# Router scores as extra columns of A's products, and z of the next group ahead of out of this one

## The chip, the cores and the metric

The kernel runs on one core of one Trainium2 chip. The metric is the device time of one execution in microseconds; lower is better. Its engines are TensorE (PE in the profile; its weight loads are listed apart as PEld), VectorE (DVE), ScalarE (ACT), GpSimd (POOL) and SyncE (SP, which here only starts DMAs). Everything is computed in 32-bit floats.

## The reference

`x` has the shape (64, 64, 1024): 64 samples, each a matrix of 64 rows (c) by 1024 columns (t). Each sample picks one of 16 matrices of 64x64. The result of that product goes through a mixture of 64 low-rank experts, 16 of them per token, and is added to x.

```
W   = weights[condition]                       # (64, 64, 64)
xf  = einsum('bct,bcd->bdt', x, W)             # conditioned rows, 4096 x 1024
scores = xf @ Wr.T                             # 4096 x 64
top_vals, top_idx = top_k(scores, 16)
G   = scatter(softmax(top_vals))               # gates, 0 where not chosen
h   = einsum('nd,krd->nkr', xf, A)             # 64 experts of rank 16 = 1024 columns
out = einsum('nkr,kdr->nd', h * G[:, :, None], B)
return x + 2.0 * out
```

The product with W works on the rows of a sample, A and Wr on the columns. So the kernel may multiply x by A first (the product is called z here) and put W on afterwards; for the scores it may do the same with Wr.

## The kernel before, in words

The 4096 rows are worked in 8 groups of 512 (four tiles of 128 rows, `TPG = 4`). A group has two large products, each 512 x 1024 by 1024 x 1024:

- z = x A (called "h" in the code, L582 on), by blocks `a_t` that stay in SBUF,
- out = h B (called "o"), by blocks `b_t`.

Each product is done by a Strassen-Winograd scheme: seven products of quarters, p1 to p7, instead of eight. They are called parents, and `parent()` makes one. At level 1 a parent is 16 matmuls of 512 columns. At level 2 each parent is itself split into seven leaves, of two matmuls each, 128 x 128 by 128 x 256. A 32-bit matmul appears in the trace as two records (passes). Group 0 is at level 1, z of group 1 has two parents at level 1 and five at level 2, and all else is at level 2. A leaf of B, and some of A's (p4, p6, p7), is computed once, written to DRAM while group 0 runs, and fetched again for every use into a ring of `RING` = 14 buffers. `mm()` (L482) issues a leaf's two matmuls and then `fetch()`, which starts the next fetch on SP's queue and waits there until the buffer is free. Leaves p1, p2, p3, p5 of A stay in SBUF. The parents' order within a product is ORDER: z goes p1 p2 p4 p6 p7 p5 p3, out goes p1 p7 p4 p6 p5 p2 p3.

`run()` (L496) writes out one parent. Its order on PE is: p1 into bank x, p2 into bank y, p3 of the parent before (the "tail"), p6 into x, p4 of the parent before, the hooks "mid", the left sums of the parent after (`prepare`, four DVE sums), the hooks "late", p7 into bank w, p5 into x, then `done` of the parent before and the hooks "end". Bank x is copied by ACT on the way (l_r after p1, l_a after p6, l_b after p5), because each of these partial sums is needed by another quarter (`copied`, L513), and `part` (L517) adds such a copy to another bank on DVE. `done` adds the finished parent to the others on DVE: for z the sums of quarters (`z_parents`), for out the addition to the residual tile, and the store of a quarter when it has all its parts.

The order of everything is written by hand (`manual_schedule`). `at(n, when, f)` hangs a step f on a hook of parent n. The steps that matter here:

- Scores. `scores_t` (L167) multiplies Router's columns (`wr_sb`) by the group's x tiles: 16 matmuls of 256 columns into `st`. `turn` (L186) brings the result to rows (four matmuls, `sp`), `scores` (L198) puts W on it (eight matmuls of 64x64, `sw`). Each has one bank of the pool `ps_s`, and one copy on ACT. The group's scores are made in the out stage of the group before: `scores_t` in its third parent, `turn` in its fourth, `scores` in its fifth.
- Routing. `route_top`, `exps` and four `rest` steps choose the 16 largest and form the exponentials. `scaled` is four ACT activations that scale them, `gates` four PE transposes (`gp`) and a copy into `gg`.
- `gated` (L284) puts W on one quarter of z: 64 records of 64x64 matmuls into two banks (`zp`), then two DVE products with the gates into `hb`, the left operand of out. The four quarters come one by one in four different parents: the fifth and the seventh of z, the first and the second of out.
- `load_x` fetches a quarter of the next group's x (512 KB); all four stand after the first parent of out. `load_res` fetches the four residual tiles, in the third parent of z (the fifth in group 1).

SBUF tiles are in pools; while group 0 runs, a part of SBUF holds the B blocks and the staging tiles, and `second_level()` gives it to the ring and the temporary tiles of the leaves (`lp`, `lt`). PSUM has 8 banks: 7 in the pool `acc`, 1 in `ps_s`. The order of the stages is z0 out0 z1 out1 z2 out2 .. z7 out7.

Of the kernel before, what the change touches and what calls it, by code (L numbers as in the profile page):

```python
# [15 lines left out]
P = 128  # L16
# [8 lines left out]
RING = 14  # L25
# [3 lines left out]
def kernel(  # L29
# [22 lines left out]

    nc = tc.nc
# [3 lines left out]
    KR = a_t.shape[1] * a_t.shape[4]  # L57
# [12 lines left out]
    mp = ctx.enter_context(tc.tile_pool(name="mp", bufs=5))  # L70
    rp = ctx.enter_context(tc.tile_pool(name="rp", bufs=4))
    acc = ctx.enter_context(tc.tile_pool(name="acc", bufs=7, space=PSUM))
    ps_s = ctx.enter_context(tc.tile_pool(name="ps_s", bufs=1, space=PSUM))
# [3 lines left out]
    bpool = first_group.enter_context(tc.tile_pool(name="bpool", bufs=1, side="right"))  # L77
    bsum = first_group.enter_context(tc.tile_pool(name="bsum", bufs=4, side="right"))
# [15 lines left out]
    def load_block(name, src, r, c, pool, parts=1):  # L94
        t = pool.tile([P, CH, BANK], F32, name=name)
        for k in range(parts):
            s = ts(k, CH // parts)
            nc.sync.dma_start(t[:, s, :], src[r, c][:, s, :])
        return t
# [10 lines left out]
    wr_sb = const.tile([P, 2 * CH, K], F32)  # L110
# [27 lines left out]
    idle = ps_s.tile([P, P], F32, tag="s", name="idle")  # L138
    for _ in range(10):
        nc.tensor.matmul(idle, lhsT=ident, rhs=ident, start=True, stop=True)  # L140
    two_i = const.tile([P, K], F32)
# [25 lines left out]
    def scores_t(st):  # L167

        g = st["g"]
        s = ps_s.tile([P, 2, HN], F32, tag="s", name=f"st_{g}")  # L170
        for h in range(2):
            for c in range(2 * CH):
                e = slice((c % 2) * K, (c % 2 + 1) * K)
                nc.tensor.matmul(  # L174
                    s[e, h, :],
                    lhsT=wr_sb[:, c, :],
                    rhs=xq[g, c // CH, h][:, c % CH, :],
                    start=(h == 0 and c < 2),
                    stop=(c >= 2 * CH - 2),
                    skip_group_check=True,  # L180
                )
        st_sb = small.tile([P, 2 * HN], F32, tag="st_sb", name=f"st_sb_{g}", bufs=1)
        nc.scalar.copy(st_sb, s.rearrange("p h n -> p (h n)"))
        st["st"] = st_sb

    def turn(st):  # L186

        g = st["g"]
        sp = ps_s.tile([P, TPG, K], F32, tag="s", name=f"sp_{g}")
        for i in range(TPG):  # L190
            nc.tensor.matmul(
                sp[:, i, :], lhsT=st["st"][:, ts(i, P)], rhs=two_i, start=True, stop=True
            )
        zr = small.tile([P, TPG, K], F32, tag="zr", name=f"zr_{g}", bufs=1)
        nc.scalar.copy(zr, sp)
        st["zr"] = zr

    def scores(st):  # L198

        g = st["g"]  # L200
        sw = ps_s.tile([P, TPG, K], F32, tag="s", name=f"sw_{g}")
        for i in range(TPG):
            for j in range(2):
                r = slice(j * C, (j + 1) * C)
                nc.tensor.matmul(
                    sw[r, i, :], lhsT=ws[g][r, i, :], rhs=st["zr"][r, i, :], start=True, stop=True
                )
# [69 lines left out]
    def gates(st):  # L277

        gp = ps_s.tile([P, TPG, P], F32, tag="s", name=f"gp_{st['g']}")
        for i in range(TPG):  # L280
            nc.tensor.transpose(gp[:, i, :], st["g2"][i].rearrange("p a k -> p (a k)"), ident)
        nc.scalar.copy(gg.rearrange("p (i n) -> p i n", n=P), gp)

    def gated(st, i, j):  # L284
# [7 lines left out]
        for c in range(CH):  # L292
            for s in range(2):
                for b in range(2):
                    r = slice(b * C, (b + 1) * C)
                    for e in range(2):
                        nc.tensor.matmul(  # L297
                            zp[b][e * D : (e + 1) * D, c, s, :],
                            lhsT=z[r, s, ds(c * P + e * D, D)],
# [54 lines left out]
    }  # L354

# [5 lines left out]
    for k in "ho":  # L361
        for j in ORDER[k]:
            for p in LEAVES:
                if k == "o" or p not in STAY:
                    leaf_d[k, j, p] = tc.dram_tile([P, 2, HALF], F32, name=f"{k}_{j}_{p}")
# [4 lines left out]
    def leaf_steps(k, j, block, pool):  # L370

        (q11, q12), (q21, q22) = quads(block, HALF)
        made = {}

# [4 lines left out]
        def step(op_, p, a, b):  # L379
            def f():  # L380
                made[p] = pool.tile([P, 2, HALF], F32, tag="leaf", name=f"{k}s_{j}_{p}")
# [33 lines left out]
    def fetch():  # L415
        if to_fetch:
            key = to_fetch.pop(0)
            t = pools["bp"].tile([P, 2, HALF], F32, tag="b", name="l{}_{}_{}".format(*key))
# [11 lines left out]
    pools = {}  # L430

    def parent(kind, st, j, level, left, whole, done):
# [4 lines left out]

        def begin():
            m = mp.tile([P, 2, BANK], F32, tag="m", name=f"m_{g}_{kind}_{j}")
            q = [[m[:, i, ts(k, HALF)] for k in range(2)] for i in range(2)]  # L440
            par.update(m=m, q=q, bank={}, val={})

        def half(s):

            b = par["bank"][s] = acc.tile(
                [P, BANK], F32, tag="acc", name=f"{kind}_{g}_{j}_{s}"
            )
            for c in range(CH):
                piece(s, c)
            nc.scalar.copy(par["m"][:, s, :], b)  # L450

        def piece(s, c):
# [3 lines left out]
                rhs=whole[j][:, c, :],  # L456
# [5 lines left out]
        def both():  # L462
# [6 lines left out]
            for s in range(2):  # L469
                nc.scalar.copy(par["m"][:, s, :], par["bank"][s])  # L470

        def prepare():
            lp = pools["lp"]
            t1, t2, t3, t4 = (
                lp.tile([P, 2, P], F32, tag=n, name=f"l_{n}") for n in ("t1", "t2", "t3", "t4")
# [8 lines left out]
        def mm(bank, p, first):  # L484
            w, v = weights(kind, j, p), par["leaf"][p]
            for c in range(2):
# [3 lines left out]
                    rhs=w[:, c, :],  # L490
# [10 lines left out]
    def run(par, before, after, hooks):  # L501
# [5 lines left out]
        def bank(n):  # L507
            par["bank"][n] = acc.tile(
                [P, HALF], F32, tag="acc", name=f"{par['kind']}_{par['g']}_{par['j']}_{n}"
# [3 lines left out]
        def copied(n):  # L513
            par["val"][n] = pools["lt"].tile([P, HALF], F32, tag=n, name=f"l_{n}")
# [22 lines left out]
        elif par:  # L537
            par["half"](0)
        if tail:
# [19 lines left out]
        if before:  # L559
            before["done"](before["m"])  # L560
# [14 lines left out]
    def z_parents(st, order, levels, whole):  # L575

        st["z"] = {}
        held, m_ = set(), {}

        def done(j):  # L580
            def f(m):
                m_[j] = m  # L582
                held.add(j)
                if j == "p2":
                    add(m, m, m_["p1"])
                    st["z"][0, 0] = m
                elif j == "p6":
                    add(m_["p1"], m_["p1"], m)
                elif j == "p3":
                    add(m_["p1"], m_["p1"], m)  # L590
                    st["z"][0, 1] = m_["p1"]
                if j == "p7":
                    assert "p6" in held
                    add(m, m, m_["p1"])
                if {"p7", "p4"} <= held and (1, 0) not in held:
                    held.add((1, 0))
                    add(m_["p4"], m_["p4"], m_["p7"])
                    st["z"][1, 0] = m_["p4"]
                if {"p7", "p4", "p5"} <= held and (1, 1) not in held:
                    held.add((1, 1))  # L600
                    add(m_["p7"], m_["p7"], m_["p5"])
                    st["z"][1, 1] = m_["p7"]
                    add(m_["p1"], m_["p1"], m_["p5"])
# [8 lines left out]
    def load_res(st):  # L612
        g = st["g"]
        st["os"] = {}
        for i, j in ((0, 0), (1, 0), (1, 1), (0, 1)):
            o = st["os"][i, j] = rp.tile([P, 2, BANK], F32, tag="o", name=f"o_{g}_{i}{j}")
# [5 lines left out]
    def o_parents(st, order, levels, whole):  # L622
# [15 lines left out]
        def late():  # L638
            if {"p2", "p5"} <= m_.keys():
                into(0, 1, m_["p5"])  # L640

        def done(j):
            def f(m):
# [9 lines left out]
                elif j == "p4":  # L653
                    into(1, 0, m, {"p7", "p6"} <= m_.keys())
                elif j == "p7":
# [18 lines left out]
    at2 = apool.tile([P, CH, BANK], F32, name="at2")  # L674
    at3 = apool.tile([P, CH, BANK], F32, name="at3")
    at4 = apool.tile([P, CH, BANK], F32, name="at4")
# [6 lines left out]
    for st in sts:  # L683
        order = ORDER if st["g"] else FIRST
        st["h"] = len(parents)
        lv = {0: (1,) * 7, 1: (1, 1, 2, 2, 2, 2, 2)}.get(st["g"], (2,) * 7)
        parents += z_parents(st, order["h"], lv, ar)
        st["o"] = len(parents)
        lv = (2,) * 7 if st["g"] else (1,) * 7
        parents += o_parents(st, order["o"], lv, br)  # L690
# [51 lines left out]

    def a_leaf(j):
        for f in leaf_steps("h", j, ar[j], pools["al"]):
            f()

    def second_level():

        first_group.close()
        for n, b in (("bp", RING), ("lp", 2), ("lt", 2), ("al", 6)):  # L750
# [44 lines left out]


    for st in sts:
        g, h, o = st["g"], st["h"], st["o"]
        nxt = sts[g + 1] if g + 1 < NG else None
        if g:  # L800
            at(h + 0, "late", rest, st, 1)
            at(h + 1, "late", rest, st, 2)
            at(h + 2, "late", rest, st, 3)
            at(h + 0, "end", sums, st, "x_sums", "s2")
            at(h + 2, "end", sums, st, "x_sums", "s1")
            at(h + 3, "end", sums, st, "x_sums", "s4")
            at(h + 2, "end", scaled, st)
            at(h + 3, "mid", gates, st)
            at(h + 4, "mid", gated, st, 0, 0)
            at(h + 6, "mid", h_operands, st)  # L810
            at(h + 6, "mid", gated, st, 1, 0)
            at(h + 6, "end", sums, st, "h_sums", "s3")
            at(o + 0, "mid", gated, st, 1, 1)
            at(o + 0, "end", sums, st, "h_sums", "s2")
            at(o + 1, "mid", gated, st, 0, 1)
            at(o + 1, "end", sums, st, "h_sums", "s1")
            at(o + 2, "end", sums, st, "h_sums", "s4")
        at(h + (4 if g == 1 else 2), "mid", load_res, st)
        if g == 1:

            at(h + 0, "mid", fetches, 5)
            at(h + 0, "end", fetches, 5)
            at(h + 1, "mid", fetches, RING - 10)
            at(h + 2, "end", a_leaf, "p1")
            at(h + 3, "end", a_leaf, "p2")
        if nxt:
            at(h + 1, "mid", gather, g + 1)
            for i, j in ((0, 0), (1, 0), (0, 1), (1, 1)):
                at(o, "end", load_x, g + 1, i, j)
            at(o + 2, "mid", x_operands, nxt)  # L830
            at(o + 2, "mid", scores_t, nxt)
            at(o + 3, "mid", turn, nxt)
            at(o + 3, "end", sums, nxt, "x_sums", "s3")
            at(o + 4, "mid", scores, nxt)
            at(o + 4, "end", route_top, nxt)
            at(o + 5, "mid", exps, nxt, 0, 1)
            at(o + 5, "end", exps, nxt, 2, 3)
            at(o + 6, "late", rest, nxt, 0)

# [47 lines left out]
```

## Time and profile before

| | |
|---|---|
| median of 3 runs | 803.16 us (802.76 to 803.45) |
| the profiled execution | 803.06 us, its span 801.0 us |
| mean granted PE clock | 0.998 of full speed |
| period of a group in the middle | 96.67 us (scores `st` at 476.14 and at 572.80 us) |
| fetches of B leaves, of A leaves | 343 and 141, of 256 KB each |
| DMA traffic | 203.91 MB, mean 255 GB/s |

Times are microseconds. A line of the timeline has the start, the duration of the merged records, the engine, the line of the kernel, the operation, output <- inputs by the program's names, the shape and the number of records merged; an idle time before it stands in brackets, with what ended it. A line of windows has the stretch, its length, then busy time and count for PE, PEld, DVE, ACT and POOL, the granted clock of PE, the DMA engines' busy share and GB/s.

### The profile page before, as it was taken

The numbers are of one execution on the slowest core, as the hardware profiler recorded it, in microseconds if no ns is written. First come the engines' busy times: TensorE is split into PE (matmuls) and PEld (weight loads), VectorE is DVE, ScalarE is ACT, GpSimd is POOL, SyncE is SP. The second block draws the span as 40 slices with busy tenths as digits, with TensorE's granted clock in tenths as the row PEclk, the third lists the DMA queues.
The fourth block names the chain that finished last, engine by engine and source line by source line (L and its number), as shares of the span: only waits on it lengthen the run. The fifth ranks groups of instructions, "written<-read, shape, count | busy, mean of one in ns | idle before, by whom it ended". The sixth has DMA issues, their size and how long they took to land.

```text
span 801.0 us, 14915 instructions
## 1 busy us (share of the span) xinstructions
PE 786.1 (98%) x5492; PEld 625.1 (78%) x5492; DVE 619.0 (77%) x1297; ACT 194.9 (24%) x512; POOL 34.3 (4%) x39
## 2 busy tenths in 40 slices
PE   8999999999999999999999999999999999999996
PEld 5444445888888888888888888888888888888885
DVE  1779797987886868768696777968788787786886
ACT  1131121322322122322223212222232222223121
POOL 4001100001000100001000010000100000000000
PEclk9999999999999999999999999999999999999999
DMA  8813779979885798848897497964978659886584
GB/s 318 339 47 132 262 264 336 327 259 322 284 281 182 240 303 306 288 133 281 282 316 258 138 326 232 353 222 145 323 243 322 223 165 336 267 291 212 181 284 159
DMA packets 113686, 203.91 MB, mean 255 GB/s; under 512 B 12112, under 2 KB 31312, under 8 KB 112720
## 3 DMA queue, kind: packets, MB, share of 16 engines
q1 hardware_dynamic: 112160, 201.11, 73.8%
q0 software_dynamic: 1024, 1.05, 0.4%
q8 instruction: 44, 0.72, 0.4%
q10 hardware_dynamic: 432, 0.82, 0.3%
q14 instruction: 26, 0.21, 0.1%
HBM read 170.16 MB, written 32.77 MB: 253 GB/s over the span
## 4 chain that ended last, share of the span: by engine, by line
PE 88%; DVE 8%; DMA 2%; ACT 1%; issue 1%; DVEq 0%; ACTq 0%
PE o_p_x L487 21%; PE h_p_x L487 19%; PE o_p_w L487 11%; PE h_p_w L487 10%; PE h_p L453 7%; PE o_p_y L487 5%; PE h_p_y L487 4%; PE zp L297 4%; PE st L174 3%; PE o_p L453 2%; DMA h_p_p<-hs_p_p 1%; DVE o L81 1%; DVE os_p_p L84 1%; DVE l_t L84 1%; DMA x<-in_x_t_dram 1%; DVE m_h_p L81 1%
## 5 line engine op out<-in xcount | busy, mean ns | idle before, releaser
L487 PE MATMUL o_p_x<-lo_p_p,l_t 128*128 128x256 f32 x584 | 143.1, 379 | 0.0
L487 PEld LDWEIGHTS o_p_x<-lo_p_p,l_t 128*128 128x128 f32 x584 | 111.2, 190 | 14.9
L81 DVE TENSOR_TENSOR o<-o,m_o_p 128x1024 f32<-128x1024 f32 (+1 forms) x73 | 86.0, 1197 | 0.6
L81 DVE TENSOR_TENSOR m_h_p<-m_h_p,m_h_p 128x1024 f32<-128x1024 f32 x56 | 67.5, 1218 | 0.3
L150 POOL DMA_INDIRECT w_st<-in_cw_dram,idx x32 | 33.6, 1049 | 536.6 <-PE zp L297 520.5
L81 DVE TENSOR_TENSOR m_h_p<-h_p_w,l_a 128x256 f32<-128x256 f32 x47 | 19.9, 423 | 45.5 <-PE h_p_w L487 45.5
L310 DVE TENSOR_TENSOR hb<-zp,gg 128x512 f32<-128x512 f32 x64 | 41.2, 686 | 17.1 <-PE zp L297 17.1
L487 PE MATMUL h_p_x<-a,l_t 128*128 128x256 f32 x208 | 53.4, 379 | 0.0
L487 PE MATMUL o_p_w<-lo_p_p,l_t 128*128 128x256 f32 x196 | 53.4, 395 | 0.0
L487 PE MATMUL h_p_x<-lh_p_p,l_t 128*128 128x256 f32 x188 | 49.0, 383 | 4.1 <-ACT l_r L515 4.1
L81 DVE TENSOR_TENSOR m_o_p<-o_p_w,l_b 128x256 f32<-128x256 f32 x49 | 20.7, 422 | 41.3 <-ACT l_b L515 41.2
L487 PE MATMUL h_p_w<-lh_p_p,l_t 128*128 128x256 f32 x188 | 49.7, 387 | 0.0
L515 ACT COPY l_b<-h_p_x 128x256 f32<-128x256 f32 x47 | 17.5, 372 | 114.7 <-PE h_p_x L487 113.3
L515 ACT COPY l_b<-o_p_x 128x256 f32<-128x256 f32 x49 | 18.2, 372 | 108.9 <-PE o_p_x L487 108.9
L487 PEld LDWEIGHTS h_p_x<-lh_p_p,l_t 128*128 128x128 f32 x188 | 35.2, 190 | 11.3 <-ACT l_r L515 6.8
L487 PEld LDWEIGHTS h_p_x<-a,l_t 128*128 128x128 f32 x208 | 39.6, 190 | 5.3
L487 PE MATMUL h_p_x<-at,l_t 128*128 128x256 f32 x168 | 43.1, 379 | 0.0
L297 PEld LDWEIGHTS zp<-w_st,m_h_p 64*64 64x64 f32 x2048 | 32.8, 135 | 11.7 <-issue 10.2
L487 PEld LDWEIGHTS o_p_w<-lo_p_p,l_t 128*128 128x128 f32 x196 | 34.7, 190 | 7.0 <-issue 2.3
L487 PEld LDWEIGHTS h_p_w<-lh_p_p,l_t 128*128 128x128 f32 x188 | 34.1, 190 | 4.7
L297 PE MATMUL zp<-w_st,m_h_p 64*64 64x64 f32 x2048 | 37.2, 221 | 0.0
L81 DVE TENSOR_TENSOR m_o_p<-o_p_w,l_a 128x256 f32<-128x256 f32 x48 | 20.3, 424 | 21.7 <-PE o_p_w L487 21.7
(147 smaller groups left out, 1387.5 us busy)
## 6 DMA issues: line engine op xcount, KB each, us to landing
lo_p_p<-o_p_p SPq DMA_DIRECT2D x280, 256.0 KB, 3.6
lh_p_p<-h_p_p SPq DMA_DIRECT2D x141, 256.0 KB, 5.3
o<-in_x_dram SPq DMA_DIRECT2D x32, 512.0 KB, 7.4
lo_p_p<-in_b_t_dram SPq DMA_DIRECT2D x63, 256.0 KB, 3.9
x<-in_x_t_dram SPq DMA_DIRECT2D x31, 512.0 KB, 6.5
out_dram<-o SPq DMA_DIRECT2D x31, 512.0 KB, 4.0
o_p_p<-os_p_p SPq DMA_DIRECT2D x28, 256.0 KB, 3.0
h_p_p<-hs_p_p SPq DMA_DIRECT2D x21, 256.0 KB, 2.4
```

The source lines that it names most:

```text
L81: nc.vector.tensor_tensor(o, a, b, ALU.add)
L84: nc.vector.tensor_tensor(o, a, b, ALU.subtract)
L150: nc.gpsimd.indirect_dma_start(out=w_st[:, i, :], out_offset=None, in_=cw, in_offset=bass.IndirectOffsetOnAxis(ap=idx[:, n : n + 1], axis=0),)
L174: nc.tensor.matmul(s[e, h, :], lhsT=wr_sb[:, c, :], rhs=xq[g, c // CH, h][:, c % CH, :], start=(h == 0 and c < 2), stop=(c >= 2 * CH - 2), ...
L297: nc.tensor.matmul(zp[b][e * D : (e + 1) * D, c, s, :], lhsT=z[r, s, ds(c * P + e * D, D)], rhs=ws[g][r, 2 * i + s, :], start=True, stop=True,
L310: nc.vector.tensor_tensor(tokens(hb[j, i])[:, :, :, b, :], zp[b], g_ij[:, :, :, b, :], ALU.mult)
L453: nc.tensor.matmul(par["bank"][s], lhsT=left()[j][:, c, ts(s, P)], rhs=whole[j][:, c, :], start=c == 0, stop=c == CH - 1, skip_group_check ...
L487: nc.tensor.matmul(bank, lhsT=v[:, c, :], rhs=w[:, c, :], start=first and c == 0, stop=c == 1, skip_group_check=True,)
L515: nc.scalar.copy(par["val"][n], par["bank"]["x"])
```

## The change

Router's transposed weight is laid beside A on the host: each quarter of a block of `a_t` gets 16 more columns (`KC = 16`), so a block has 2 x 272 columns instead of 512. From group 2 on, a z parent at level 2 works on 272 columns instead of 256, and the last 16 of each half of z are the scores before W. `scores` then reads them from z, with 16 matmuls of 64x64 by 32 columns; `scores_t` and `turn` stay for groups 0 and 1. The A blocks' sums, the staged and fetched leaves of A and z's tiles grow with them.

The order of the stages becomes z0 out0 z1 z2 out1 z3 out2 .. z7 out6 out7. From group 2 on, a group's z is complete one out stage earlier than before, and its routing is done in that out stage: `scores` and `route_top` in its second parent, `exps` in the third, the `rest` steps after (the last one in the first parent of the following z stage). `scaled` and `gates` stand in one parent, the second of the following z stage (for the last group the sixth of out6), at its hooks "mid" and "late". `gated` is called in pairs: quarters (0,0) and (1,0) at the end of that parent, (1,1) and (0,1) in the middle of the next (for the last group the first of out7).

The x tiles of the next group are loaded one by one in the fourth to the seventh parent of z, the residual tiles in the z stage before their out stage (for the last group around the turn from out6 to out7). All 8 PSUM banks are in one pool. The ring has 13 buffers; z parents have a pool of their own (`zp`, 6 tiles, also used to stage the leaves of p1 and p2 of A), out parents 3 tiles instead of 5; these and the residual tiles lie in SBUF where group 0 had its blocks and staging.

The diff, cut to its core:

```diff
-RING = 14
+RING = 13
+KC = 16
...
-    acc = ctx.enter_context(tc.tile_pool(name="acc", bufs=7, space=PSUM))
-    ps_s = ctx.enter_context(tc.tile_pool(name="ps_s", bufs=1, space=PSUM))
+    acc = ctx.enter_context(tc.tile_pool(name="acc", bufs=8, space=PSUM))
...
     def scores(st):
...
+                for k in range(2):
+                    nc.tensor.matmul(
+                        sw[r, i, ts(k, K // 2)].rearrange("p (d k) -> p d k", d=2),
+                        lhsT=ws[g][r, i, :],
+                        rhs=halves(st["z"][i // 2, k])[r, i % 2, :, HALF:],
+                        start=True,
+                        stop=True,
+                    )
...
+    WIDTH = {"h": HALF + KC, "o": HALF}
...
+        width = WIDTH[kind] if g > 1 else HALF
...
                 nc.tensor.matmul(
                     bank,
                     lhsT=v[:, c, :],
-                    rhs=w[:, c, :],
+                    rhs=w[:, c, :width],
...
+    for k, g in (
+        [("h", 0), ("o", 0), ("h", 1)]
+        + [(k, n) for g in range(2, NG) for k, n in (("h", g), ("o", g - 1))]
+        + [("o", NG - 1)]
+    ):
...
-        for n, b in (("bp", RING), ("lp", 2), ("lt", 2), ("al", 6)):
+        for n, b in (("bp", RING), ("lp", 2), ("lt", 2), ("zp", 6), ("mp", 3), ("rp", 4)):
...
+    for st in sts[2:]:
+        n = st["h"] + 7
+        last = st["g"] + 1 == NG
+        at(n + 1, "mid", scores, st)
+        at(n + 1, "late", route_top, st)
+        at(n + 2, "mid", exps, st, 0, 1)
+        at(n + 2, "end", exps, st, 2, 3)
+        slots = (2, 3, 3, 4) if last else (3, 5, 6, 7)
+        for i in range(TPG):
+            at(n + slots[i], "late" if i == (1 if last else 3) else "end", rest, st, i)
+        at(n + (5 if last else 8), "mid", scaled, st)
+        at(n + (5 if last else 8), "late", gates, st)
+        m = n + (5 if last else 8)
+        at(m, "end", gated, st, 0, 0)
+        at(m, "end", gated, st, 1, 0)
+        m = n + (7 if last else 9)
+        at(m, "mid", gated, st, 1, 1)
+        at(m, "mid", gated, st, 0, 1)
...
+    QUARTERS = ((1, 0), (1, 1), (0, 0), (0, 1))
...
+            if g > 1:
+                at(h - 1, "mid", x_operands, st)
+                at(h + 1, "mid" if g == 2 else "late", sums, st, "x_sums", "s3")
...
+            for k, q in enumerate(QUARTERS):
+                at(o - 2 + k if g + 1 == NG else o - 4, "mid", load_res, st, q)
+            if g + 1 < NG:
+                at(h + 3, "mid", gather, g + 1)
+                at(h + 3, "end", load_x, g + 1, 0, 0)
+                at(h + 4, "end", load_x, g + 1, 1, 0)
+                at(h + 5, "mid", load_x, g + 1, 1, 1)
+                at(h + 6, "mid", load_x, g + 1, 0, 1)
...
-    def in_blocks(t):
-        return t.reshape(2, CH, P, 2, BANK).transpose(0, 3, 2, 1, 4)
+    def in_blocks(*ts_):
+        parts = [t.reshape(2, CH, P, 2, 2, -1).transpose(0, 3, 2, 1, 4, 5) for t in ts_]
+        return np.concatenate(parts, -1).reshape(2, 2, P, CH, -1)
```

Here h and o are the positions of a group's first z parent and first out parent in the list of parents.

## The prediction

> **What bounds the kernel now.** I read the page first: totals, then the chain that ended last.
>
> ```profile
> span 801.0 us, 14915 instructions
> PE 786.1 (98%) x5492; PEld 625.1 (78%) x5492; DVE 619.0 (77%) x1297; ACT 194.9 (24%) x512; POOL 34.3 (4%) x39
> ...
> PE 88%; DVE 8%; DMA 2%; ACT 1%; issue 1%; DVEq 0%; ACTq 0%
> ```
>
> PE is busy 98% and carries 88% of the chain; weight loads (PEld) are at 78% and lie beside the matmuls. So a pass taken from PE or added to it moves the end one for one, unless another engine can no longer keep up. Next, the timeline of PE in group 5, to price each block by the starts around it.
>
> ```profile
> 460.44 1.02 PE L487 MATMUL h_p_w<-lh_p_p,sum_p 128*128 128x256 f32 x4
> 461.40 1.16 PE L297 MATMUL zp<-w_st,m_h_p 64*64 64x64 f32 x64
> ...
> 463.46 1.03 PE L487 MATMUL o_p_x<-lo_p_p,l_t 128*128 128x256 f32 x4
> ...
> 475.11 1.03 PE L487 MATMUL o_p_w<-lo_p_p,hb 128*128 128x256 f32 x4
> 476.06 3.67 PE L174 MATMUL st<-x,wr_sb 128*64 128x256 f32 x32
> 479.67 1.13 PE L487 MATMUL o_p_w<-lo_p_p,l_t 128*128 128x256 f32 x4
> 480.64 1.03 PE L487 MATMUL o_p_x<-lo_p_p,l_t 128*128 128x256 f32 x4
> ...
> 484.95 1.02 PE L487 MATMUL o_p_w<-lo_p_p,hb 128*128 128x256 f32 x4
> 485.82 1.00 PE L191 MATMUL sp<-two_i,st_sb 128*128 128x64 f32 x8
> ...
> 487.57 1.03 PE L487 MATMUL o_p_x<-lo_p_p,l_t 128*128 128x256 f32 x4
> ```
>
> A record is one of a matmul's two passes; x4 is one leaf (two matmuls). Undisturbed leaves start 0.864 us apart, so a pass of 256 columns is 0.216 us. What a guest costs is the distance between two leaf starts around it, less 0.864 per leaf between: Router scores st 480.64-475.11-1.73 = 3.80; turn sp 487.57-484.95-1.73 = 0.89; one gated quarter zp 463.46-460.44-1.73 = 1.29. Likewise sw (491.89 to 494.43) is 0.81 and the transposes gp (529.92 to 532.09) 0.44. In the same timeline:
>
> ```profile
> 527.23 1.03 PE L487 MATMUL h_p_x<-at,l_t 128*128 128x256 f32 x4
> 528.95 1.13 PE L487 MATMUL h_p_x<-lh_p_p,l_t 128*128 128x256 f32 x4 [0.69 <-ACT l_r L515]
> 529.92 1.03 PE L487 MATMUL h_p_w<-lh_p_p,x 128*128 128x256 f32 x4
> ```
>
> Here PE loses 529.92-527.23-1.73 = 0.96: ACT does the four `scaled` activations (1.28 us from 527.37) ahead of l_r, which p6 waits for. The account closes: 98 leaves x 0.864 = 84.7, plus 3.80+0.89+0.81+0.44+4x1.29+0.96 = 12.1, is 96.7; the group's period is 96.67 (st at 476.14, next at 572.80). So PE never waits elsewhere in a group. Last, the windows of an out and a z stage, and of DMA's busiest 6 us:
>
> ```profile
> 456.30:507.40 51.10, 51.10 (x385) 43.29 (x385) 40.75 (x79) 12.82 (x35) 3.83 (x4) 1.00 0.82 275
> 507.40:553.00 45.60, 44.91 (x326) 38.90 (x325) 34.73 (x91) 12.06 (x33) 0.00 (x0) 1.00 0.70 237
> 661.00:667.00 6.00, 6.00 (x88) 5.09 (x87) 4.75 (x11) 1.12 (x3) 0.00 (x0) 1.00 1.02 399
> ```
>
> DVE (third count) has about 10 us free per stage; DMA (last two) has room on average.
>
> **The change, step by step**, against the profiled run: 803.06 us, 2.06 around a span of 801.0; the median of the runs is 803.16, so the two agree.
>
> 1. Router apart, removed. Groups 2 to 7 lose st and sp: 6 x (3.80+0.89) = -28.1 us. Groups 0 and 1 keep theirs. Their two ACT copies go too, off the path.
>
> 2. Wider A leaves. In groups 2 to 7 each z leaf is 272 columns: 49 leaves x 2 matmuls x 2 passes = 196 passes a group, 1176 in all. 16 columns more at 0.216/256 are 0.0135 us: +15.9. The trace has no 272. Bounds: 0, were a pass set by its weight load (190 ns, so no: 256 columns already take 216); and 0.0139 us from the 512-wide passes of group 0 (32 in 13.93 us, 0.435 each), +16.3. I take 15.9. The copies and adds on ACT and DVE grow by a sixteenth, some 1 us a group inside DVE's 10 free.
>
> 3. Paired quarters. Of a zp's 1.29, 1.09 is its 64 matmul records and 0.20 switching in and out. Two in a row pay that once: groups 1 to 7, two pairs each, 14 x -0.20 = -2.8 (bound 0, if the switch sits between quarters).
>
> 4. `scaled` and `gates`. `scaled` moves from an "end" to a "mid" hook, so l_r's wait goes: 7 x -0.96 = -6.7. But the transposes now stand "late" in the same run, from group 2 on. From that run's p6 end: ACT starts l_a 0.25 later, it takes 0.33, four activations 1.28, so the last transpose ends near 2.0; unhindered (p4, 0.92, then 0.44) it would end at 1.36. PE, with p7 queued behind, waits 0.66: 6 x 0.66 = +4.0. Net -2.7; ends -6.7 (if all is hidden) and +2 (if each wait is 1.4).
>
> 5. `scores` from z. sw takes 16 matmuls of 32 columns for 8 of 64, and moves to p7 of the out stage before. The nearest row, sw's 16 records in 0.71 us, is 44 ns a record: 32 would take 1.41, +0.70. If columns set it, +0. I take +0.35, 6 x = +2.1 (0 to 4.2). The Trainium skill speaks against the split: "TensorE: Matmul & The Clock Gate", Back-to-back issue gap, gives 1 to 64 columns the same cost, about 60 cycles. By that rule the term is its upper end, +4.2, and the total 2.1 higher. sw waits for p3's add into z's quarter 0,1, queued on DVE a run's first part (4.3 us) before: covered.
>
> 6. Order and queues. x loads move from the out stage to z (each when its tile has had its last reader), residual loads to the z stage before their out stage, route_top, exps and rest to the out stage. SP's fetches stand behind these loads; in z the ring uses 3 leaves in 6.4 us, so 13 buffers are over 25 us of cover. In the out stage DVE needs, by steps in its timeline, 7 prepares x 1.47, 21 part adds x 0.34, 14 adds of 1.13 and 4.0 of routing: 37.2 us, of 43.3+1.2 of PE. Covered by 7 us; the fullest runs (a `rest` beside two adds, 5.8 of 6.04) have no more than the run at 508.7 to 514.7, where DVE had 0.17 us free and PE did not wait.
>
> 7. Start. A's blocks are 1088 KB for 1024; the chain starts with x's 6.27 us DMA and a11. DVE's A sums and staged leaves grow by a sixteenth in a stage where DVE is already late (PE waits 0.93 for `b` at 107.75). Tiles of z, out parents and residuals now lie over group 0's memory, so z1's first ACT copy may wait for the last b leaf (DVE 128.5, copy 125.23). PE has PSUM for two runs ahead. I take +1, bounds -2 and +6.
>
> 8. End. out6 and out7 follow each other, with four residual loads in SP's queue, each behind a store (4.0 us to land) started about 2.5 us before: some 2.5 us of SP per run, beside 7 fetches at 0.42. Fits in 6.04 barely; +1, bounds 0 and the second rival's 11.
>
> Sum: -28.1+15.9-2.8-2.7+2.1+1+1 = -13.6; 803.06-13.6 = 789.5, rounded to 789.
>
> **Rivals.** (a) All hidden: 4 at -6.7, 5 at 0, 7 and 8 at 0: -21.7, 781. Against: the transposes do follow their activations within a run.
>
> (b) The last pair of out stages is bound by transfers. In 77 us it moves 85 leaves (22.3 MB), about five stores and four residual loads (4.7 MB): 27 MB, less 3.4 in the ring at its start. At the 275 GB/s of the former out stage that takes 86 us, +9, with SP's waits up to +11: 792 to 800. Against: that rate was demand, since 6 us windows show 399, 387 and 380, and the start's loads 368 to 405 for 21 us (14 to 35). The Trainium skill ("DMA: Bandwidth & Descriptors", Specifications) puts HBM per core at about 358 GB/s. By it the pair needs 66 us and fits; the windows of 380 to 405 here exceed it, so the measurement stands.
>
> (c) PSUM turns the sign. Now a quarter holds two of seven banks; the pair holds four of eight while x and w of the run are still live, and the next run's x and y take the last two. If a reused bank is one that DVE's hb product has yet to read, PE waits for it each time: two products 1.29 us plus the wait to start, up to 2.7 per pair, 14 pairs: +38, so 803 to 827. It decides from 13.6/14 = 1.0 us per pair. For it: no bank is spare. Against: after zp at 461.40, p7 took a new bank and started 1.09 later with no wait, so banks just read are not the ones reused, and the pair finds banks drained a run earlier.
>
> (d) Wider passes and the new waits cancel what leaves: within 0.2%, 1.6 us, about what a measurement of this kernel can tell from no change. It asks for 12 us more that no row names.
>
> **How the numbers follow.** My forecast, 783.5 to 792, 0.63; (a) 781 to 783.5, 0.05; (b) 0.18; (d) 0.03; (c) 0.11. Faster is 0.63+0.05+0.18 = 0.86, same 0.03, slower 0.11. Range 783.5 to 798: outside it lie (a), (d), (c) and perhaps 0.01 of (b), 0.2 in all. Its floor is the forecast with steps 4 and 5 at their good ends (789.5-4.0-2.1 = 783.4), its roof (b) without its last 2 us.
>
> **What the next profile would show.** st and sp 64 and 16 records instead of 256 and 64; z leaves of 128x272 at starts 0.918 apart; a period of 96.67-4.69+2.65-0.40-0.96+0.66+0.35 = 94.3 between equal blocks of two groups; zp of 128 records in 2.4; PE idle before gp near 0.7, for ACT's g; no wait for l_r. I am wrong if 272 columns cost more than 0.0135, if PE waits for `hb` (c) or for leaves after out6 (b), or if PE idles over 3 us between 60 and 175.

## The result and the profile after

| | before | after |
|---|---|---|
| median | 803.10 us (802.76 to 803.45, 4 runs) | 790.63 us (789.21 to 791.95, 4 runs) |
| the profiled execution, its span | 803.06, 801.0 | 790.09, 788.0 |
| period of a group in the middle | 96.67 | 94.00 |
| DVE busy | 619.0 (77%) | 626.8 (80%) |

The ratio is 0.9844, interval 0.9826 to 0.9863. In a later series of runs the changed kernel gave 790.01 (789.37 to 791.51, 5 runs) and a ratio of 0.9833 [0.9816, 0.985]. Line numbers have moved: L530 is now `mm`, L318 `gated`, L298 `gates`, L286 `scaled`, L218 `scores`, L448 `fetch`, L671 the residual loads, L685 a store. (The starts of st in before are 476.06 and 572.73, as its timeline line shows; 476.14 and 572.80 are 0.08 late, and the period is the same.)

The page of after, the lines that answer to those shown of before (span, totals, chain by engine):

```profile
span 788.0 us, 14615 instructions
PE 774.4 (98%) x5348; PEld 608.9 (77%) x5348; DVE 626.8 (80%) x1297; ACT 191.7 (24%) x500; POOL 36.8 (5%) x39
PE 83%; DVE 9%; DMA 6%; issue 1%; SPq 0%; ACT 0%; DVEq 0%
```

PE is still the bound, at 98%. It is busy 11.7 us less, which is nearly all of the gain. The timeline of PE in after, in the z stage of group 5 and the out stage after it (start, duration, engine, line, operation, shape, records):

```profile
455.67 1.08 PE L530 MATMUL h_p_w<-lh_p_p,x 128*128 128x272 f32 x4
456.61 1.20 PE L298 MATMUL gp<-ident,g 128*128 128x128 f32 x4
457.65 1.08 PE L530 MATMUL h_p_w<-lh_p_p,l_t 128*128 128x272 f32 x4
458.57 1.08 PE L530 MATMUL h_p_x<-a,l_t 128*128 128x272 f32 x4
459.58 2.09 PE L318 MATMUL zp<-w_st,m_h_p 64*64 64x64 f32 x128
461.60 1.18 PE L530 MATMUL h_p_x<-at,x 128*128 128x272 f32 x4
462.62 1.08 PE L530 MATMUL h_p_y<-at,x 128*128 128x272 f32 x4
...
473.10 1.08 PE L530 MATMUL h_p_x<-lh_p_p,l_t 128*128 128x272 f32 x4
474.01 1.08 PE L530 MATMUL h_p_w<-lh_p_p,x 128*128 128x272 f32 x4
...
505.62 1.03 PE L530 MATMUL o_p_w<-lo_p_p,hb 128*128 128x256 f32 x4
506.57 1.14 PE L218 MATMUL sw<-m_h_p,w_st 64*64 64x32 f32 x32
507.64 1.13 PE L530 MATMUL o_p_w<-lo_p_p,l_t 128*128 128x256 f32 x4
508.61 1.03 PE L530 MATMUL o_p_x<-lo_p_p,l_t 128*128 128x256 f32 x4
```

Prices as in the prediction, a distance of starts less the leaves between. A z leaf is 0.917, the mean over several starts (474.01-473.10 is one). The transposes: 457.65-455.67-0.917 = 1.06 where gp alone was 0.44, so PE lost 0.62. That loss has no bracket: gp's four records stand for 1.20 us, because each follows one activation of `scaled` (1.28 us on ACT from 456.15). A wait can hide inside a group of records that lasts too long. A pair of quarters: 462.62-458.57-2x0.917 = 2.21, for 2.58 as two singles. sw: 508.61-505.62-2x0.864 = 1.26, for 0.81.

In the last two out stages PE waits three times where before it did not; the timeline again, idle time and releaser in brackets:

```profile
719.05 1.03 PE L530 MATMUL o_p_w<-lo_p_p,sum_p 128*128 128x256 f32 x4
721.50 1.21 PE L298 MATMUL gp<-ident,g 128*128 128x128 f32 x4 [1.42 <-ACT g L286]
722.54 1.03 PE L530 MATMUL o_p_w<-lo_p_p,l_t 128*128 128x256 f32 x4
...
741.66 1.03 PE L530 MATMUL o_p_y<-lo_p_p,hb 128*128 128x256 f32 x4
743.49 1.99 PE L530 MATMUL o_p_x<-lo_p_p,l_t 128*128 128x256 f32 x8 [0.80 <-issue]
745.32 1.03 PE L530 MATMUL o_p_w<-lo_p_p,hb 128*128 128x256 f32 x4
...
755.68 1.89 PE L530 MATMUL o_p_x<-lo_p_p,l_t 128*128 128x256 f32 x8
757.76 1.10 PE L530 MATMUL o_p_w<-lo_p_p,hb 128*128 128x256 f32 x4 [0.19 <-DMA lo_p_p<-o_p_p]
758.70 1.03 PE L530 MATMUL o_p_w<-lo_p_p,l_t 128*128 128x256 f32 x4
```

The first costs 2.19 in all (722.54-719.05-0.864-0.44): from `scores` to `scaled` the last group has four parents of out6 where the others have seven, and DVE starts to write `invs`, which `scaled` reads, only at 720.84. The second costs 1.07 (745.32-741.66-3x0.864) and had its leaf in SBUF 7.9 us before. The third costs 0.43 (758.70-755.68-3x0.864) and is a leaf from the ring that landed late.

### The profile page after: what moved, and what is told of

It is laid out like the page before. It is cut to its first block, busy times and chain, and to the rows that moved or that the text cites. A ratio compares the mean times of both kernels' runs of the same rounds, so it can differ in the third digit from the quotient of the medians.

```text
span 788.0 us, 14615 instructions
## 1 busy us (share of the span) xinstructions
PE 774.4 (98%) x5348; PEld 608.9 (77%) x5348; DVE 626.8 (80%) x1297; ACT 191.7 (24%) x500; POOL 36.8 (5%) x39
## 4 chain that ended last, share of the span: by engine, by line
PE 83%; DVE 9%; DMA 6%; issue 1%; SPq 0%; ACT 0%; DVEq 0%
PE h_p_x L530 21%; PE o_p_x L530 19%; PE h_p_w L530 11%; PE o_p_w L530 10%; PE h_p_y L530 5%; PE h_p L495 5%; PE o_p_y L530 5%; PE zp L318 4%; DMA h_p_p<-hs_p_p 2%; DVE o L84 2%; DVE os_p_p L87 2%; DMA o_p_p<-os_p_p 1%; PE gp L298 1%; DMA out_dram<-o 1%; DVE hs_p_p L87 1%
## 5 line engine op out<-in xcount | busy, mean ns | idle before, releaser
L530 PE MATMUL o_p_x<-lo_p_p,l_t 128*128 128x256 f32 x584 | 143.0, 379 | 0.8 <-issue 0.8
L530 PEld LDWEIGHTS o_p_x<-lo_p_p,l_t 128*128 128x128 f32 x584 | 110.8, 190 | 16.6 <-issue 1.2
L84 DVE TENSOR_TENSOR m_h_p<-m_h_p,m_h_p 128x1088 f32<-128x1088 f32 (+1 forms) x56 | 70.3, 1267 | 5.5 <-ACT m_h_p L492 5.2
L84 DVE TENSOR_TENSOR m_h_p<-h_p_w,l_a 128x272 f32<-128x272 f32 (+1 forms) x47 | 20.6, 438 | 57.1 <-PE h_p_w L530 57.0
L153 POOL DMA_INDIRECT w_st<-in_cw_dram,idx x32 | 36.0, 1125 | 530.4 <-PE zp L318 513.9
L530 PE MATMUL h_p_x<-a,l_t 128*128 128x272 f32 (+1 forms) x208 | 55.9, 391 | 0.0
L530 PE MATMUL h_p_w<-lh_p_p,l_t 128*128 128x272 f32 (+1 forms) x188 | 51.2, 395 | 0.0
L530 PE MATMUL o_p_w<-lo_p_p,l_t 128*128 128x256 f32 x196 | 51.0, 383 | 0.0
L530 PE MATMUL h_p_x<-lh_p_p,l_t 128*128 128x272 f32 (+1 forms) x188 | 50.5, 391 | 0.0
L564 ACT COPY l_b<-h_p_x 128x272 f32<-128x272 f32 (+1 forms) x47 | 18.1, 385 | 118.8 <-PE h_p_x L530 118.8
L530 PEld LDWEIGHTS h_p_x<-a,l_t 128*128 128x128 f32 x208 | 39.5, 190 | 7.8
L530 PE MATMUL h_p_x<-at,l_t 128*128 128x272 f32 (+1 forms) x168 | 45.0, 390 | 0.0
L530 PEld LDWEIGHTS h_p_x<-lh_p_p,l_t 128*128 128x128 f32 x188 | 35.7, 190 | 6.9
L530 PEld LDWEIGHTS o_p_w<-lo_p_p,l_t 128*128 128x128 f32 x196 | 36.6, 190 | 5.1
L530 PEld LDWEIGHTS h_p_w<-lh_p_p,l_t 128*128 128x128 f32 x188 | 35.0, 191 | 6.5
L318 PEld LDWEIGHTS zp<-w_st,m_h_p 64*64 64x64 f32 x2048 | 31.7, 135 | 7.8 <-issue 6.9
L530 PEld LDWEIGHTS h_p_x<-at,l_t 128*128 128x128 f32 x168 | 31.9, 190 | 6.3
L318 PE MATMUL zp<-w_st,m_h_p 64*64 64x64 f32 x2048 | 34.3, 220 | 0.3 <-issue 0.3
```

Of the source, the lines that this page charges most:

```text
L84: nc.vector.tensor_tensor(o, a, b, ALU.add)
L153: nc.gpsimd.indirect_dma_start(out=w_st[:, i, :], out_offset=None, in_=cw, in_offset=bass.IndirectOffsetOnAxis(ap=idx[:, n : n + 1], axis=0),)
L318: nc.tensor.matmul(zp[b][e * D : (e + 1) * D, c, s, :], lhsT=halves(z)[r, s, c // 2, ds(c % 2 * P + e * D, D)], rhs=ws[g][r, 2 * i + s, :] ...
L530: nc.tensor.matmul(bank, lhsT=v[:, c, :], rhs=w[:, c, :width], start=first and c == 0, stop=c == 1, skip_group_check=True,)
L564: nc.scalar.copy(par["val"][n], par["bank"]["x"])
```

## The experiments

All differ from the changed kernel or from another experiment by the edit shown.

**1. Router apart, everything else as changed.** Does the gain come from the wider leaves, or from order and pairs?

```diff
-KC = 16
+KC = 0
...
+        b = st["h"] + 1 if st["g"] == 2 else st["h"] - 5
+        at(b, "mid", scores_t, st)
+        at(b + 1, "mid", turn, st)
...
```

(The rest puts Router's own tiles into other pools and one x sum of group 2 one hook later.)

> The order, the pairs, the hooks and the pools of the changed kernel, but Router's scores apart again (KC = 0, scores_t and turn for every group). Theory of the prediction: PE pays for what it is given. Six groups get st and sp back (6 x 4.69 = +28.1 us) and lose the 16 columns (294 leaves x 0.053 = -15.6) and half of sw (6 x -0.45 = -2.7): +9.8 on 790.6, so 800.4. Rival: the gain is the order's and the pairs', and the columns cost as much as st and sp did: 790.6 within 1.6.

Measured 803.0 (800.6 to 805.34, 10 runs), ratio 1.0003 [0.999, 1.0016]. The period is 95.66, as expected to 0.02, so the block prices hold: -28.1 + 15.6 + 2.7 is what Router's columns are worth. The time is 2.6 above the forecast. The trace shows where it went: waits of 0.8 (h_p_x for DVE's hb) and 0.7 (issue at a zp) that stand once, and 1.6 us right behind the wait for gp, where two leaves ran at half the clock (see the last experiment). With a z1 that starts 0.9 later than in before and the 2.19 for gp these are 6.2 us, about the 6 x 1.0 that the periods give. So order and pairs without the wider leaves do nothing for the time.

**2. Quarters one by one.** Pairs undone, in group 1 too: each quarter in a parent of its own.

```diff
...
-        at(m, "end", gated, st, 1, 0)
-        m = n + (7 if last else 9)
-        at(m, "mid", gated, st, 1, 1)
-        at(m, "mid", gated, st, 0, 1)
+        at(m + 1, "mid", gated, st, 1, 0)
+        at(m + 2, "mid", gated, st, 1, 1)
+        at(m + 3, "mid", gated, st, 0, 1)
```

> The four quarters of z go through W one by one in four parents, as in the kernel before, all else as in the changed kernel. Theory: each of 14 pairs saved 0.37 us of PE (two singles cost 2 x 1.29, a pair 2.21): +5.2 us, 795.8; less up to 1.5 if the waits without a releaser (0.97 us at 743.5, 0.6 at 367.4) come from 256 PE instructions in 2.1 us that a pair asks for. Rival: pairs cost PE waits for PSUM or DVE, so singles are no slower: 790 or less.

Measured 794.94 (793.36 to 795.97), ratio 0.9896 [0.988, 0.9913]. The period is 94.71 = 94.00 + 2 x 0.36. Its timeline, a single quarter:

```profile
461.13 1.08 PE L530 MATMUL h_p_x<-a,l_t 128*128 128x272 f32 x4
462.14 1.16 PE L318 MATMUL zp<-w_st,m_h_p 64*64 64x64 f32 x64
463.23 1.19 PE L530 MATMUL h_p_x<-at,x 128*128 128x272 f32 x4
```

A single takes 1.09 from its start to the next leaf's, a pair 2.02 (459.58 to 461.60): the second 64 records cost 0.93, not 1.09. So a pair saves the switch (0.20) and 0.16 besides.

**3. The transposes behind p7 and p5.** Takes PE's wait for ACT's activations away by asking for their result a third of a parent later.

```diff
-        at(n + (5 if last else 8), "late", gates, st)
+        at(n + (5 if last else 8), "end", gates, st)
```

> The transposes of the gates moved from the hook late to the hook end of the same parent, so that p7 and p5 run while ACT does the four activations. Theory: PE stops waiting for ACT there: 5 x 0.62 and, in the last group, most of 2.19, so -4 to -5.3 us, 785.3 to 786.6. Rival: the wait only moves, to the gated products behind the copy gg or to the next parent's sums: 790.6 within 1 us.

Measured 785.55 (785.14 to 786.26), ratio 0.9786 [0.9769, 0.9802], a period of 93.37 = 94.00 - 0.63. In its timeline gp is 0.60 long and nothing waits:

```profile
456.80 1.08 PE L530 MATMUL h_p_x<-a,l_t 128*128 128x272 f32 x4
457.71 0.60 PE L298 MATMUL gp<-ident,g 128*128 128x128 f32 x4
458.24 2.10 PE L318 MATMUL zp<-w_st,m_h_p 64*64 64x64 f32 x128
```

So 5 x 0.62 + 2.19 = 5.3 us of the changed kernel's time was this one kind of wait, and one word of the schedule takes it out (5.1 by the medians).

**4. Six PSUM banks instead of eight**, for rival (c).

```diff
-    acc = ctx.enter_context(tc.tile_pool(name="acc", bufs=8, space=PSUM))
+    acc = ctx.enter_context(tc.tile_pool(name="acc", bufs=6, space=PSUM))
```

> Two of the eight PSUM banks left out. Theory: a bank that the gated products have just read is drained by DVE before PE comes back to it (0.1 to 0.3 us late per pair at most): 790.6 to 795. Rival: the pair leaves no bank spare with eight, so with six every pair waits for two products of DVE, 1.3 us and more: 14 x 1.3 = +18, 809 and up.

Measured 792.33 (791.6 to 795.43), ratio 0.9881 [0.9861, 0.9901]. The period stays at 94.00 with two banks fewer. Only in the last group does PE wait for a bank that `hb` still reads:

```profile
729.43 1.13 PE L530 MATMUL o_p_x<-lo_p_p,sum_p 128*128 128x256 f32 x4 [1.94 <-DVE hb L331]
```

This is rival (c)'s mechanism, at 1.9 us, once. It also stands once in experiment 1, which has all eight banks:

```profile
280.93 1.13 PE L530 MATMUL h_p_x<-at,x 128*128 128x256 f32 x4 [0.79 <-DVE hb L331]
```

In after there is no such wait behind group 0, so (c) falls as an account of the changed kernel.

**5. More DMA traffic**, for rival (b): behind every fourth fetch of a B leaf, 256 KB copied within DRAM, some 85 copies.

```diff
...
+            if key[0] == "o":
+                spare.append(key)
+                if len(spare) % 4 == 0:
+                    d = tc.dram_tile([P, 2, HALF], F32, name=f"spare_{len(spare)}")
+                    nc.sync.dma_start(d, leaf_d[key])
```

> The changed kernel with a quarter more fetch traffic: after every fourth fetch of a B leaf, a copy of that leaf, 256 KB, from DRAM to DRAM, that nobody reads. An out stage moves 17.8 MB instead of 14.6. Theory: the stages in the middle have room in DMA and the ring, so PE does not wait there; the last pair, where the ring was nearly empty, loses some us: 791 to 805. Rival (transfers already set the out stages' time): 22.3 MB more at some 350 GB/s, +64: 840 and up.

Measured 794.0 (792.99 and 795.0, 2 runs), ratio 0.9881 [0.9859, 0.9904]. Windows of the last two out stages, first of after, then of this kernel (stretch, length, busy time and count of PE, PEld, DVE, ACT, POOL, granted clock, DMA share, GB/s):

```profile
703.00:780.00 77.00, 74.53 (x578) 63.76 (x577) 63.99 (x139) 19.14 (x52) 0.00 (x0) 1.00 0.90 308
```
```profile
703.00:780.00 77.00, 72.09 (x567) 62.01 (x566) 62.97 (x138) 18.99 (x53) 0.00 (x0) 1.00 1.01 356
```

Even this load costs 3.4 us over the changed kernel's median. PE's waits for leaves, 4.2 us in the trace, all lie in out7, where the DMA engines are now full. So transfers do not bound the middle, and in the pair of out stages after has some room in the mean. "DMA: Bandwidth & Descriptors", Specifications, in the Trainium skill gives 358 GB/s for a core; the 356 here, with leaves late, stands close to that, though it is no test of it, since a copy within DRAM both reads and writes there, and in before single windows showed up to 405. After's late leaf at 757.76 had another cause, next.

**6. Residual loads of the last group on GpSimd's queue**, on top of experiment 3. SP's own waits in after, from 700 to 770 (total, times, longest):

```profile
SPq L448 <- PE o_p_x L530: 9.2, 22, 0.8
SPq L671 <- DMA out_dram<-o: 7.5, 3, 3.7
```

The first line is the ring at work: a fetch waits for a free buffer. The second is SP standing before a residual load until the store that held its tile has landed, up to 3.7 us, with all fetches behind it.

```diff
+            queue = nc.gpsimd if g + 1 == NG else nc.sync
-            nc.sync.dma_start(
+            queue.dma_start(
```

> The gates at the hook end, and the last group's four residual loads issued by GpSimd's queue instead of SyncE's. Theory: in out7 the ring runs short because each residual load holds SP's queue until a store has landed (3.7 to 9 us); off that queue the fetches are early again and PE's waits for leaves near 747 to 758 us (0.4 to 0.9) go: 785.55 - 0.4 to 1.2, so 784.4 to 785.2. Rival: the last two out stages are bound by the transfers themselves; the same bytes in the same time leave the ring as short: 785.5 or more.

Measured 783.68 (783.06 to 784.09), ratio 0.9753 [0.9739, 0.9766]. That is 1.9 under its base, which ran on another chip, and below what was expected: by the traces 0.9 is the wait for a leaf, and 0.7 a shorter wait near 144 that the edit does not touch. On one chip, the two kernels of experiment 7 differ by this edit alone, and their medians by 1.8. No wait for a leaf is left. By issue and landing in the trace, after's leaves from 752 to 762 landed 0.1 to 1.3 us before their use, here 1.1 to 2.8. SP's queue, not bandwidth alone, had thinned the ring.

**7. The two leaf steps of z1's third parent, later.** In experiment 3's kernel one long wait is left, 1.63 us for bank w near 144, where DVE does two 128x544 subtractions ahead of the add that frees the bank. They are moved behind it, on top of experiment 3 alone and together with experiment 6:

```diff
-        at(h + n, "mid" if n == 1 else "late", steps_of, late_steps, 2)
+        at(h + n, "mid" if n == 1 else "end", steps_of, late_steps, 2)
```

> The gates at the hook end, and in z of group 1 two staged leaf steps of A moved from the hook late to the end of the third parent. Theory: near 142 us PE waits 0.5 to 1.9 us because the sum that empties bank w stands behind these steps on DVE, so p4 of that parent is late; with the steps behind the sum the wait goes: 785.55 - 0.7 to 1.9, so 783.7 to 784.9. Rival: DVE is late there as a whole (group 0's staging), and the wait moves to the next parent: 785.5 within 0.5.

> Gates at the hook end, leaf steps at the end, residual loads of the last group by GpSimd's queue. Theory: the three act at three places and add up: 785.55 - 1.1 to 3.1, so 782.5 to 784.5. Rival: one of them only moves a wait: 785 and up.

Measured 786.32 (785.21 to 786.53) alone, 784.48 (783.97 to 786.59) together: no gain, and a miss. The wait for w is gone, but 2.15 and 2.27 us stand at 150 to 151 instead. DVE's own waits from 125 to 165, first in experiment 6's kernel, then in the second kernel here, name what had been overlooked:

```profile
DVE hs_p_p L87 <- DMA h_p_p<-hs_p_p: 1.6, 2, 1.1
```
```profile
DVE hs_p_p L87 <- DMA h_p_p<-hs_p_p: 2.0, 2, 1.5
DVE m_h_p L84 <- DMA h_p_p<-hs_p_p: 1.2, 1, 1.2
```

The leaves that DVE stages take their buffers from the pool of z's parents, and wait until earlier ones have been written to DRAM; in the second kernel a sum of a z parent (`m_h_p`) waits for that too.

**8. Staged leaves of p2 in the idle pool `mp`**, then also the later steps.

```diff
...
-        late_steps.extend(leaf_steps("h", j, ar[j], pools["zp"], "z"))
+        n, tag = ("mp", "m") if j == "p2" else ("zp", "z")
+        late_steps.extend(leaf_steps("h", j, ar[j], pools[n], tag))
```

> Base: the version with the gates at "end" and the last residual loads on GpSimd's queue (783.7). The three staged leaves of A's p2 take tiles of the out parents' pool mp (3 tiles, unused until out1) instead of zp, so that they no longer wait for p1's staged leaves to reach DRAM. Theory (in the base, DVE's waits for those DMAs, 0.50 at 142.10 and 1.09 at 145.01, delay the adds that PE's p4 and p7 wait for, 0.93 at 143.97): the wait of PE near 144 falls under 0.5, the time is 782.7 to 783.3. Rival (DVE is simply full there; the wait is its work): the wait stays near 0.9 and so does the time, 783.5 to 784.1. In both, DVE's line 'hs_p_p <- DMA h_p_p<-hs_p_p' goes from 1.6 to near 0.

> As the kernel with p2's staged leaves in mp, and the two leaf steps of the hook "late" in z1's third parent stand at "end", behind the adds that free bank w. Alone this move had only carried the wait on (to 150 and 151, 2.15 to 2.27 for m_h_p). Theory (that new wait came from DVE standing before the staged leaves' buffers): with the buffers free it is gone, PE waits under 0.5 in all between 140 and 155, 782.5 to 783.1. Rival (DVE's work there is simply later than PE by then): a wait of 1 to 2.3 near 151 again, 784 to 785.

Measured 782.65 (782.1 to 783.05), ratio 0.9738 [0.9723, 0.9753], and 782.45 (781.7 to 783.12), ratio 0.9736 [0.9721, 0.9752]. PE's waits of the first (0.4 for bank w), then all that the view lists for the second:

```profile
PE h_p_w L532 <- DVE m_h_p L84: 0.4, 1, 0.4
```
```profile
PE idle L143 <- POOL ident masks.py:199: 1.5, 1, 1.5
PE o_p L497 <- DVE b L87: 0.7, 1, 0.7
PE o_p L497 <- DVE hb L87: 0.4, 1, 0.4
```

DVE's waits for those writes are gone in both. With the buffers free the same move that had failed leaves no wait of PE behind group 0. The gain of 1 us over experiment 6 is from runs on different chips, and the two versions here are not told apart. 782.45 is the shortest time measured: 7.6 under the changed kernel on the same chip.

**9. The changed kernel again**, beside those two.

> The changed kernel itself once more, beside these two on the same chip, since its runs had spread over 2.7 us (789.2 to 791.95) where the kernel before spreads over 0.7. If the spread is its own, these runs lie between 789 and 792 with a median near 790.5; if it was one chip's, they lie within 0.7 of each other.

Measured 790.01 (789.37 to 791.51): as expected for a spread of its own. But the kernel before spread over 802.35 to 805.02 beside it, so a spread of 2 to 3 us is not peculiar to the change. One part of it can be read. This profile shows what after's didn't, right behind the wait for gp (timeline, then windows; the granted clock is the third figure from the end):

```profile
721.27 1.29 PE L298 MATMUL gp<-ident,g 128*128 128x128 f32 x4 [1.42 <-ACT g L286]
722.36 1.92 PE L530 MATMUL o_p_w<-lo_p_p,l_t 128*128 128x256 f32 x4
724.06 1.83 PE L530 MATMUL o_p_x<-lo_p_p,l_t 128*128 128x256 f32 x4
725.82 2.09 PE L318 MATMUL zp<-w_st,m_h_p 64*64 64x64 f32 x128
```
```profile
722.20:725.70 3.50, 3.50 (x9) 2.52 (x9) 0.71 (x3) 0.59 (x1) 0.00 (x0) 0.51 0.96 270
```

Two leaves start 1.70 and 1.76 apart instead of 0.864: at half the clock for some 3.4 us, a loss of 1.7. In after's trace the same stretch has a clock of 1.00 behind the same 1.42 us of waiting.

## Why the prediction was right

Forecast 789, range 783.5 to 798; measured 790.63. By the profiled runs the sum said -13.6 and 13.0 came (801.0 to 788.0). By its steps:

1. **Router apart removed, -28.1.** Right: 64 records of st and 16 of sp are left, and experiment 1 puts its cost back to 0.02 of a period.
2. **Wider leaves, +15.9.** Right: 0.917 - 0.864 = 0.053 a leaf, 294 leaves, +15.6. (The upper bound was misread: undisturbed 512-wide passes start 0.429 apart, not 0.435, which gives 0.0134 for 16 columns and +15.8.)
3. **Pairs, -2.8.** Mis-sized: -0.37 a pair, so -5.2 over 14. The term counted the switch alone and took 64 records at 1.09 for both; the second 64 took 0.93. Even its bounds, -2.8 and 0, did not hold this.
4. **`scaled` and `gates`, net -2.7.** Two errors. The l_r wait was taken seven times; in the trace of before it stands in groups 2 to 7 only, so -5.8 (6 x 0.96). And the new wait for ACT's g was right at 0.66 in the middle (0.62), but taken for the last group too, where it was 2.19, because `rest` on DVE is late there. The last group's schedule is a case of its own, and its steps had not been followed. Together +5.3, net -0.5.
5. **`scores` from z, +2.1.** +0.45 each, +2.7. The rule of the Trainium skill ("TensorE: Matmul & The Clock Gate", Back-to-back issue gap) that 1 to 64 columns cost the same would have made it 4.2, by the prediction's estimate; 32 records of 32 columns took 1.07 from start to next leaf, 33 ns each, where 16 of 64 columns took 0.71, 44 ns each. These are means over whole blocks of different length, with the switch to the next leaf inside, so they do not test the rule for one record.
6. **Order and queues, 0.** One wait for issue in the middle of a zp pair (0.6 at 367) and no other between groups 2 and 6.
7. **Start, +1.** z1's first level-2 leaf came 0.87 earlier, and the wait for bank w at 142.88 took 0.76 back: -0.1. The wait that was named, of z1's first ACT copy for a b leaf, does not show on PE; what held z1 up was the new pool's buffers, by way of DVE's staged leaves (experiments 7 and 8).
8. **End, +1.** The leaf at 757.76 (0.43), the wait for issue at 743.49 (1.07) and 0.31 more from PE's last record to the end of the span (6.87 before, 7.18 after): +1.8. The mechanism written down (SP behind stores) is what experiment 6 shows; of the size, over half was the wait for issue, which no step had.

These sum to -28.1 + 15.6 - 5.2 - 0.5 + 2.7 + 0.6 - 0.1 + 1.8 = -13.2; 0.2 stays open. So the number came out close because steps 3 and 4 erred by 2.4 and 2.2 in opposite senses, which was luck. The sign rested on steps 1 and 2, and these were read off rows.

Of the rivals, (a) at 781 is nearly what the kernel can do once the waits that step 4, 7 and 8 name are gone (782.45). (b) as a bound by transfers falls with experiment 5, (c) with experiment 4. The sign of being wrong that was written down for (b), a wait for leaves after out6, did show, once and for 0.43 us; experiment 6 puts it down to SP's queue.

The cause of the waits for issue was not tested, but the traces point to one. They list 43 or 44 instruction fetches of 16 KB over the span, about 1 us each. In all four gaps that end with "issue" PE goes on 1.46 to 1.56 us after such a fetch has ended: in after at 367.35 (fetch to 365.89) and 743.49 (742.01), in experiment 1 at 752.85 (751.29), in experiment 5 at 369.42 (367.88). Three of the four lie inside a zp pair, behind 125 of its 128 records, each of which has a weight load: 256 PE instructions in 2.1 us. For one pair the loss also follows the fetch. It is the first of group 3, at 364.96 in after; the fetch ended 0.93, 1.03, 0.58 and 0.18 us after the pair began in after and in experiments 5, 9 and 4, and the pair lost 0.61, 0.80, 0.24 and 0 us. (The 0.24 has no bracket: it hides in a block that is 2.34 long instead of 2.09.) No run moved a fetch, and most fetches, one within a pair of experiment 1 among them, cost nothing.

## What to carry to other kernels

Price a block by the distance between undisturbed neighbours, and look at the duration of its own records too: a wait inside a group of records has no bracket. Where a step of one engine feeds another, ask for the result one slot later before anything else; here that one word was worth 5 us more, on top of the 12.5 that the change had brought. When a wait is moved and comes back elsewhere, look at what the waiting engine itself waits for: the buffers of a shared pool were behind it, and the edit that had failed was harmless once they were free. And follow the first and the last group by themselves.

## What the runs showed of the hardware

**Half clock behind a short wait.** In four of the profiled runs PE's granted clock fell to half for 3.41 us just behind a wait: experiments 1, 2 and 9 after 1.4 us for gp, and the second kernel of experiment 7 after 2.3 us near 151. Each loses up to 1.7 us more than the wait. In after, in experiments 4 and 5 and in the first kernel of experiment 7, with the same or similar waits, it did not fall. "TensorE: Matmul & The Clock Gate", Part 1, in the Trainium skill has a free-running window of about 3.4 us by which PE's clock is halved, after an idle window. The traces agree on the length and on the free running: all four stretches start a whole number of 3.413 us after the clock first rose (in experiment 9: 722.26 - 5.46 = 716.80 = 210 x 3.413). They do not agree that a whole window must be idle. Cut each trace into these windows and add up, as an estimate from the starts of the records, the time in each without PE work: the four windows before a fall hold the most of all thirteen traces, 2.14 to 2.19 us. The next hold 2.10, 2.03 (both in experiment 5) and 2.00 (experiment 4), and the clock stays up. So it seems to matter how much of a wait falls into one window: in after the window ended at 722.00, inside the gp block, and held 1.86. No run moved a wait against the windows to test this. The versions without a wait over 1 us behind group 0 (experiments 6 and 8) show no such stretch in their traces before PE's work ends.

**More records in a row are cheaper.** 64 records of 64x64 take 1.09 us alone, and 0.93 behind 64 others (2.02 for the pair, experiment 2).
